# A sorted piece of 131072 edges in two pieces of 65536, the first of them gathered while the second is sorted

## The chip, the cores and the metric

The kernel runs on one core of a Trainium2 chip. The core has a matrix engine (PE, with its weight loads shown as PEld), a vector engine (DVE), a scalar engine (ACT), a general engine (POOL) and a queue engine (SP). Each engine takes its own instructions in a written order and waits for others through semaphores. SP, ACT and POOL also issue DMAs, each in the order of its own queue; a gather or a scatter by a list of row numbers (an indirect DMA) is issued by POOL. The time is device microseconds of one execution. Before the change it is 2055.23 us, the median of 11 runs from 2052.35 to 2058.8.

## The reference, cut to what matters

```python
edge_index = jnp.stack([src, dst])            # 200000 edges, 6250 nodes, D = 256
xn = _layernorm(x)
neigh = xn[dst]                               # one row of 256 for every edge
w = sigmoid(relu(neigh @ W1 + b1) @ W2 + b2)
num = segment_sum(neigh * w, src)             # per node: weighted sum of its edges' rows
den = segment_sum(w, src)
x = x + where(den > 0, num / max(den, 1e-12), 0) + mix(xn)
x = x + ffn(layernorm(x))                     # 6 experts of 3 layers, all run, the best 2 summed
```

The weight of an edge depends on its `dst` node alone, so the kernel makes a row of `xn * w` with `w` and a 1 behind it once for each node, and the edges only have to gather and add these rows. `mix` is an attention without softmax: one 32 by 32 matrix for each of 8 heads, summed over all nodes, and then applied to each node.

## The kernel before, in words

The nodes make 49 tiles of 128, in 13 groups of 4 tiles, and 25 blocks of 2 tiles (the block is what `blk` counts). A row of the table `y_rows` holds three bf16 terms of 258 numbers, whose sum is close to float32.

The edges come sorted by `dst`. They are cut into ranges that are treated differently:

- Edges 0 to 65535 (the piece "b", `hot`) end in the first nodes. They are sorted by source, and for each block a matrix of counts is made of comparisons (L964, L966), with products on PE (L973, L992). Nothing is gathered for them.
- Edges 65536 to 196607 (the piece "a", `cold`, 128 rows of 1024) are sorted by source with a bitonic sort on DVE (L250, L265, L266: one step is a minimum and a maximum over half the elements); between phases the data is turned on PE and copied back by ACT (L301, L302). The sorted list is written to memory, and for each block a window of it is loaded back: 44 columns of 128 edges, of which half 0 of the block uses columns 0 to 22 and half 1 uses columns 19 to 43. One column and half makes one *cold step*: a gather of 128 rows (L728, once for each column), a comparison on DVE that makes a 128 by 128 matrix `hot1` (L736), and three products on PE that add the rows to the node tile's sum `pu` (L750). There are 1175 cold steps and 1079 gathers.
- The last 3392 edges (`few`) are not sorted. For each of 27 lots of 128 edges, rows are gathered (L492), edges with equal source are added up by a product (L508), copied (L512), and added to a table in memory by a scatter (L513). Each scatter waits for the one before it, since both add to the same table.

The instructions are put in order by a planner written in the kernel: a `Line` is a generator that issues some instructions and yields the estimated busy time and a wait; `run` takes the first line in a list that is due. With this the program is laid out in two parts.

*The first part.* SP loads the piece's edges, all of `x` into one tile `xn_all` (L395), the few edges, and zeroes the table with 50 writes (L420), in this order. Then run, one beside the other: the statistics of the 49 node tiles on DVE (`deviations`, L431 and L432), the rows of `y_rows` in two interleaved lines of groups (`node_rows`), the sort of "a", the 27 few lots (`few_edges`) once the node rows are done, and what fits of the sort of "b". After the sort of "a" the first window is decoded, and a second loop places one cold step after another with `heads` (the sums for `mix`: L838, L844, L856), the rest of the sort of "b" and `equal_keys` beside them. Gathers are made 10 steps ahead (`AHEAD`) into 24 buffers (`GBUF`). This loop ends when all of those lines are done.

*The second part.* The class `Work` goes through the groups: `node_terms` (L1017), the count matrices of the blocks, the sums, the normalisation and the router, and the experts (L1145, L1162). One cold step is placed, then as much of this work as a running credit allows, so that 150 us of work (`LAST`) is left when the cold steps end. A cold step is not placed while `HELD - 2` finished sums wait for their block.

Of the kernel before, what the change touches and what calls it, by code (L numbers as in the profile page):

```python
# [20 lines left out]
GT = 4  # L21
# [6 lines left out]
GBUF = 24  # L28
AHEAD = 10
HELD = 16  # L30
# [19 lines left out]
def kernel(  # L50
# [61 lines left out]
    cold = [Piece("a", 65536, 1024, P, 44, 23, 19)]  # L112
# [79 lines left out]
    sq_ps = sps.__enter__()  # L192

    sp_small = ctx.enter_context(tc.tile_pool(name="srt", bufs=1))
    srt = tc.tile_pool(name="srt_a", bufs=1)
    sp_large = srt.__enter__()
# [8 lines left out]
    def pool_of(p):  # L205
        return sp_large if p.row == 1024 else sp_small
# [98 lines left out]
    def merged(p, k, m):  # L305

        t = turned(p, k, "t", False)
        yield 0, TURN[p.name]
# [12 lines left out]
        yield 0, TURN[p.name]  # L321
# [9 lines left out]
    TURN = {"a": 3500.0, "b": 2300.0, "c": 1600.0}  # L331
# [5 lines left out]
    def sort(p, between=()):  # L337
# [3 lines left out]
        for step_between in between:  # L341
            step_between()
# [18 lines left out]
    def starts_of(i0, i1):  # L361
        n = i1 - i0
# [9 lines left out]

    xn_pool = tc.tile_pool(name="xn", bufs=1, side="right")
    xnp = xn_pool.__enter__()
    xn_all = xnp.tile([P, NTILE, D], FP, name="xn_all")
# [18 lines left out]
    for g, t0, nt, rows, r in groups:  # L394
        nc.sync.dma_start(xn_all[:r, t0 : t0 + nt], x[t0 * P : t0 * P + rows].rearrange("(t p) d -> p t d", p=r))  # L395
# [28 lines left out]
    def deviations():  # L424
# [3 lines left out]
        for t in range(NTILE):  # L428
            r = rows_of(t)
            st = nw.tile([P, 6], FP, name="st", bufs=2)  # L430
            nc.vector.bn_stats(st[:r], xn_all[:r, t])  # L431
            nc.vector.bn_aggr(mv[:r, t], st[:r])  # L432
            yield 500, 0
# [50 lines left out]
    def few_edges():  # L484
# [3 lines left out]
        def gather(i):  # L488
            if i < NFEW:
                r = min(P, E - FEW - i * P)  # L490
                gt = nw.tile([P, TERMS, W], BF, name="gt_c", bufs=3)
# [28 lines left out]

    def node_rows(line):

        for g, t0, nt, rows, r in groups[line::2]:
            xg = xn_all[:r, t0 : t0 + nt]
# [37 lines left out]
            sq = nw.tile([P, CB, GT * P], FP, name=f"sq{line}")  # L562
            nc.scalar.activation(sq[:, 0, :rows], dev[:, :rows], AF.Square)
            nc.tensor.matmul(dev[:, :rows], centre, xnT[:, :nt, 1, :r], start=True, stop=True)

# [10 lines left out]
            nc.scalar.activation(sq[:, 1, :rows], dev[:, :rows], AF.Square)  # L576
            for j in range(nt):
                for c in range(CB):
                    nc.tensor.matmul(  # L579
                        ph[:r, P + (j * CB + c) * HB4 : P + (j * CB + c + 1) * HB4],  # L580
                        sq[:, c, j * P : j * P + r], head_of, start=True, stop=True,
                    )
# [48 lines left out]
    ORDERED = {getattr(mybir.EngineType, e) for e in ("PE", "DVE", "Activation", "Pool", "SP")}  # L631
    line_s = Line(counts(0))
    line_t = Line(few_equals(), before=[line_s])
    line_d = Line(deviations())
    lines_y = [Line(node_rows(i), before=[line_d]) for i in range(2)]
    line_c = Line(few_edges(), before=lines_y + [line_t])
    line_a = Line(sort(cold[0], [lambda: starts_of(0, 1)]))
    line_u = Line(counts(1), before=lines_y)
    line_b = Line(sort(hot))
    with tc.manual_schedule(engines=ORDERED):  # L640
        clock[0] = 4000.0
        run([line_s, line_a], 20000.0)
        first_lines = [line_s, line_d] + lines_y + [line_c, line_t, line_a]
        while any(a.open for a in first_lines):
            run(first_lines + [line_u, line_b], clock[0] + 1000.0)
    n_work.__exit__(None, None, None)
    srt.__exit__(None, None, None)
    xn_pool.__exit__(None, None, None)

# [763 lines left out]
```

## Time and profile before

| | |
|---|---|
| median of 11 runs | 2055.23 us (2052.35 to 2058.8) |
| the profiled execution's own time | 2055.01 us |
| its span, first to last instruction | 2053.2 us |
| mean granted PE clock | 0.915 |
| first gather of the cold steps issued at | 401.8 us |
| first `node_terms` result taken by DVE (second part begins) | 511.9 us |
| last gather issued at | 1828.1 us |
| busy: PE, DVE, POOL, ACT | 86%, 63%, 54%, 26% of the span |

The profile is one execution. It lists the busy time of each engine in equal slices and in chosen windows, groups of instructions by line and shape with the mean time of one, the waits in front of them, and the chain of work that ended last. The line numbers are those of the kernel before unless said otherwise. The mean of one instruction runs from its start to its end; where instructions follow each other, the next starts before the last has ended, so the distance from start to start is shorter.

### The profile page before, as it was taken

What the parts mean: (1) busy time and instruction counts of PE and PEld (TensorE: products, weight loads), DVE (VectorE), ACT (ScalarE), POOL (GpSimd) and SP (SyncE); (2) the same over time, 40 slices, a digit from 0 to 9 for tenths busy, and PEclk for the clock granted to TensorE, in tenths of its full rate; (3) what the DMA queues carried; (4) which work ended last, traced back from release to release, by engine and by line L of the source; (5) the groups of instructions that cost most, each with busy time, mean ns of one, the idle gap of its engine ahead of it and who ended that gap; (6) DMA issues with size and microseconds to landing.
All of it is one profiled execution on the core that took longest, in us unless ns stands there. A gap on an engine that the chain in (4) does not pass through costs nothing.

```text
span 2053.2 us, 29846 instructions
## 1 busy us (share of the span) xinstructions
PE 1768.1 (86%) x9751; PEld 1193.0 (58%) x9751; DVE 1300.5 (63%) x5161; ACT 531.4 (26%) x1037; POOL 1111.8 (54%) x1146
## 2 busy tenths in 40 slices
PE   0888332396888999999999999999999999999997
PEld 0555222274554676666766666666666666666555
DVE  8987899677874555566655556655656565565321
ACT  6665431000111212212121221312122122222332
POOL 0000255277777777776776767677676767740000
PEclk9866555598897999999999999999999999999999
DMA  9432233397666666565665656566565565640000
GB/s 245 136 114 93 58 62 65 96 289 228 176 165 179 164 167 193 154 190 145 178 171 150 189 145 186 147 161 190 151 192 140 156 178 157 193 99 18 1 11 14
DMA packets 148725, 294.83 MB, mean 144 GB/s; under 512 B 27914, under 2 KB 94483, under 8 KB 148563
## 3 DMA queue, kind: packets, MB, share of 16 engines
q0 software_dynamic: 74592, 222.62, 40.9%
q1 hardware_dynamic: 63719, 64.97, 10.0%
q10 hardware_dynamic: 10252, 5.27, 1.0%
q8 instruction: 78, 1.28, 0.3%
q14 instruction: 84, 0.69, 0.1%
HBM read 259.37 MB, written 33.40 MB: 143 GB/s over the span
## 4 chain that ended last, share of the span: by engine, by line
PE 76%; DVE 10%; DMA 7%; issue 3%; ACT 3%; POOL 0%; POOLq 0%; SPq 0%; DVEq 0%; ACTq 0%
PE px L1145 24%; PE pu L750 17%; PE px L1162 12%; PE ph L973 6%; PE ph L992 5%; DMA table<-sm,few_row 5%; PE ph L546 2%; PE px L1132 1%; PE ph L579 1%; DMA gt<-y_rows,dsts 1%; PE ph L1017 1%; PE px L1052 1%; DVE k_a L265 1%; DVE fr L966 1%; PE ph L856 1%
## 5 line engine op out<-in xcount | busy, mean ns | idle before, releaser
L728 POOL DMA_INDIRECT gt<-y_rows,dsts x1079 | 1033.8, 958 | 420.6 <-issue 153.7
L750 PE MATMUL pu<-gt,hot 128*128 128x258 bf16 x3525 | 576.5, 278 | 12.6 <-DMA gt<-y_rows,dsts 11.3
L750 PEld LDWEIGHTS <-hot 128*128 128x128 bf16 x3525 | 346.4, 99 | 343.2 <-issue 273.6
L966 DVE TENSOR_SCALAR fr<-count,rdl 128x128 bf16<-128x128 bf16 x1105 | 274.3, 273 | 95.5 <-PE ph L973 94.7
L1154 ACT ACTIVATE h<-px,eb_t 128x512 f32<-128x512 f32 (+1 forms) x312 | 206.6, 662 | 434.6 <-PE px L1145 433.7
L1145 PE MATMUL px<-fT,ew_t 128*128 128x512 f32 (+1 forms) x624 | 298.2, 573 | 0.3 <-ACT fT L1046 0.3
L1145 PE MATMUL px<-h,ew_t 128*128 128x512 f32 (+1 forms) x624 | 296.9, 570 | 0.0
L1162 PE MATMUL px<-ew_t,h 128*128 128x256 f32 (+1 forms) x1176 | 296.7, 380 | 0.0
L736 DVE TENSOR_SCALAR hot<-count,loc 128x128 bf16<-128x128 bf16 x1175 | 272.1, 271 | 24.9 <-PE pu L750 23.5
L1171 DVE SCALAR_TENSOR_TENSOR acc<-px,gate,acc 128x256 f32<-128x256 f32 (+1 forms) x294 | 128.5, 477 | 180.5 <-PE px L1162 180.5
L973 PE MATMUL ph<-to,fr 128*128 128x256 bf16 x1105 | 224.4, 280 | 18.0 <-DVE fr L966 15.8
L1162 PEld LDWEIGHTS px<-ew_t,h 128*128 128x128 f32 (+1 forms) x1176 | 203.4, 190 | 24.9 <-issue 4.3
L964 DVE TENSOR_SCALAR to<-count,hloc 128x256 bf16<-128x256 bf16 x562 | 168.2, 302 | 3.1 <-PE ph L973 3.1
L973 PEld LDWEIGHTS <-fr 128*128 128x128 bf16 x1105 | 108.3, 98 | 65.4 <-DVE fr L966 41.9
L975 ACT CAST cn<-ph 128x256 bf16<-128x256 f32 x150 | 55.8, 372 | 328.2 <-PE ph L973 322.5
L992 PE MATMUL ph<-yh,cn 128*128 128x258 bf16 x882 | 130.8, 273 | 0.0
L783 POOL IOTA last_first<- 128x6 f32 x1 | 0.2, 152 | 219.5 <-DVE rest L588 219.5
L1002 DVE TENSOR_TENSOR cs<-ph,cs 128x258 f32<-128x258 f32 x49 | 20.9, 427 | 153.4 <-PE ph L992 152.7
L1145 PEld LDWEIGHTS px<-fT,ew_t 128*128 128x128 f32 x624 | 96.4, 191 | 22.0 <-issue 14.7
L1145 PEld LDWEIGHTS px<-h,ew_t 128*128 128x128 f32 x624 | 95.7, 190 | 21.6 <-issue 17.1
L992 PEld LDWEIGHTS <-cn 128*128 128x128 bf16 x882 | 85.7, 97 | 15.4 <-issue 2.0
L265 DVE TENSOR_TENSOR k_a<-k_a 128x512 f32<-128x512 f32 x115 | 79.4, 691 | 4.8 <-ACT k_a L302 1.8
(227 smaller groups left out, 1668.3 us busy)
## 6 DMA issues: line engine op xcount, KB each, us to landing
gt<-y_rows,dsts POOLq DMA_INDIRECT x1079
y_rows<-ys SPq DMA_DIRECT2D x10, 774.0 KB
table<-zero SPq DMA_DIRECT2D x50, 129.0 KB
tb<-table SPq DMA_DIRECT2D x49, 129.0 KB
xn_all<-in_x_dram SPq DMA_DIRECT2D x12, 512.0 KB
xnT_d<-xnT SPq DMA_DIRECT2D x12, 512.0 KB
xt<-xnT_d SPq DMA_DIRECT2D x12, 512.0 KB
u<-in_x_dram SPq DMA_DIRECT2D x12, 512.0 KB
```

Source lines behind the costliest of these rows:

```text
L265: nc.vector.tensor_tensor(lo, a, b, op=ALU.min)
L728: nc.gpsimd.indirect_dma_start(out=gt.rearrange("p k w -> p (k w)"), out_offset=None, in_=y_rows, in_offset=bass.IndirectOffsetOnAxis(ap=d ...
L736: nc.vector.tensor_scalar(hot1, count[:, half * P : (half + 1) * P], loc[:, j : j + 1], None, op0=ALU.is_equal)
L750: nc.tensor.matmul(self.pu, hot1, gt[:, k], start=(start and k == 0), stop=(stop and k == TERMS - 1))
L964: nc.vector.tensor_scalar(made[j1], count, loc[:, j1 : j1 + 1], None, op0=ALU.is_equal)
L966: nc.vector.tensor_scalar(fr, count[:, :P], rdl[:, d1, j1 : j1 + 1], None, op0=ALU.is_equal)
L973: nc.tensor.matmul(pa, matrices[i], made[j], start=(j == j0), stop=(j == j1 - 1))
L992: nc.tensor.matmul(pu[:, :W], cn[:, d, s * P : (s + 1) * P], yh[:, d, k], start=(d == 0 and k == 0), stop=(d == HOT - 1 and k == TERMS - 1),)
L1145: nc.tensor.matmul(ph[:, :rows], w[:, e, c, f * P : (f + 1) * P], ins[:, c, :rows], start=(c == 0), stop=(c == CB - 1),)
L1154: nc.scalar.activation(h[:, f, :rows], ph[:, :rows], AF.Relu, bias=bc)
L1162: nc.tensor.matmul(po[:r, j - j0], h2[:, c, j * P : j * P + r], ew_t[2][:, e, c, :], start=(c == 0), stop=(c == CB - 1),)
L1171: nc.vector.scalar_tensor_tensor(acc[:r, j, :], po[:r, j - j0], gate[:r, j, e : e + 1], acc[:r, j, :], op0=ALU.mult, op1=ALU.add)
```

## The change

The piece "a" becomes two pieces "a" and "c" of 128 rows of 512. Each has windows of 23 columns, of which half 0 uses columns 0 to 11 and half 1 uses columns 9 to 22.

The order of cold steps becomes a list of `passes`. The first 4 blocks (`LEAD`) are gone through from "a" alone, then the same 4 blocks from "c" alone, where the partial sums kept in `parts` are added by DVE, and from block 4 on each block is gone through from both windows together. The second piece's sort is finished, in the written order, at the latest when the first window of "c" is loaded (`piece_sorted`).

The few edges leave the first part: they are now a line beside the first cold steps, and use the cold steps' gather buffers. A new loop places one cold step for every 2200 ns of planned time until they are done; then the expert weights are loaded (now on SP's queue, no longer on ACT's), and the old loop goes on with 1300 ns until the sorts of "c" and "b", `heads` and `equal_keys` are done.

`xn_all` goes. `x` is loaded group by group, once for `deviations` and once more for `node_rows` (`x_load`, four buffers of a group). These loads are issued where `deviations` begins, which is after the 50 table writes on SP's queue. The squares for the heads share the buffer `hT`, so the products of the first half of a row (`squares`) come before the second half is squared. `GBUF` goes from 24 to 22, `HELD` from 16 to 18.

```diff
-    cold = [Piece("a", 65536, 1024, P, 44, 23, 19)]
+    cold = [Piece("a", 65536, 512, P, 23, 12, 9), Piece("c", 131072, 512, P, 23, 12, 9)]
...
-    for g, t0, nt, rows, r in groups:
-        nc.sync.dma_start(xn_all[:r, t0 : t0 + nt], x[t0 * P : t0 * P + rows].rearrange("(t p) d -> p t d", p=r))
+    def x_load(g):
+        if g >= len(groups):
+            return None
+        _, t0, nt, rows, r = groups[g]
+        xs = nw.tile([P, GT, D], FP, name=f"xs{g % 2}", bufs=2)
+        nc.sync.dma_start(xs[:r, :nt], x[t0 * P : t0 * P + rows].rearrange("(t p) d -> p t d", p=r))
+        return xs
...
+    passes = [(blk, [p]) for p in cold for blk in range(LEAD)] + [(blk, cold) for blk in range(LEAD, NBLK)]
...
             if stop:
+                blk, ps = passes[i]
+                t = blk * SB + half
+                if ps == cold[1:]:
+                    self.sums[t] = self.parts.pop(t)
+                    nc.vector.tensor_tensor(self.sums[t], self.pu, self.sums[t], op=ALU.add)
+                else:
+                    (self.sums if ps == cold else self.parts)[t] = cs = csp.tile([P, W], FP, name="cs")
+                    nc.scalar.copy(cs, self.pu)
...
     with tc.manual_schedule(engines=ORDERED):
-        clock[0] = 4000.0
-        run([line_s, line_a], 20000.0)
-        first_lines = [line_s, line_d] + lines_y + [line_c, line_t, line_a]
+        clock[0] = 8000.0
+        line_u[1].before = line_u[2].before = lines_y
+        first_lines = [line_d] + lines_y + [line_u[0], line_a, line_t]
         while any(a.open for a in first_lines):
-            run(first_lines + [line_u, line_b], clock[0] + 1000.0)
+            run(first_lines + [line_u[1], line_h, line_a2, line_u[2], line_b], clock[0] + 1000.0)
+        starts_of(0)
...
+        cold_edges = Cold(lambda p: p is cold[0] or piece_sorted(p))
+        beside = [line_c, line_u[1], line_h, line_a2, line_u[2], line_b, line_e]
+        run(beside[1:], clock[0] + 9000.0)
+        cold_edges.decode(0)
+        run(beside[1:], clock[0] + 2000.0)
+        due = clock[0]
+        while line_c.open:
+            cold_edges.step()
+            clock[0] += 200.0
+            due = max(due + 2200.0, clock[0])
+            run(beside, due)
...
-                nc.scalar.dma_start(t[:, e], w[e].rearrange("(c p) h -> p c h", p=P))
+                nc.sync.dma_start(t[:, e], w[e].rearrange("(c p) h -> p c h", p=P))
```

## The prediction

> **What bounds the kernel now.** I read the slices first, then the busy time of the engines in windows cut at the events of the program (end of the statistics, last node row, first gather, start of the second part, first expert, last gather), then the groups, then single stretches.
>
> The second and fifth part of the page, and the busy time in windows (columns: length, PE, PEld, DVE, ACT, POOL, granted clock, DMA share, GB/s):
>
> ```profile
> PE   0888332396888999999999999999999999999997
> DVE  8987899677874555566655556655656565565321
> POOL 0000255277777777776776767677676767740000
> ...
> 25.00:51.00 26.00, 0.02 (x1) 0.05 (x1) 24.33 (x100) 19.32 (x32) 0.00 (x0) 1.00 0.93 246
> 51.00:225.00 174.00, 139.19 (x557) 95.49 (x558) 147.78 (x340) 100.78 (x201) 0.15 (x1) 0.74 0.32 108
> 225.00:402.00 177.00, 50.71 (x210) 36.23 (x209) 150.27 (x303) 43.83 (x102) 76.51 (x55) 0.53 0.35 66
> 402.00:512.00 110.00, 83.43 (x636) 71.18 (x636) 83.01 (x270) 6.21 (x13) 84.48 (x84) 0.89 0.82 253
> 512.00:645.00 133.00, 105.88 (x682) 70.43 (x682) 92.09 (x476) 14.21 (x39) 98.89 (x104) 0.81 0.61 169
> 700.00:1855.00 1155.00, 1150.51 (x6622) 768.98 (x6621) 694.91 (x3272) 260.57 (x500) 808.59 (x848) 1.00 0.60 164
> ```
>
> Two parts with two limits are to be seen. From 645 us PE is full (1150.5 of 1155), so there only PE work counts. Up to 512 us DVE is the fullest, 425 us busy in all; PE's spare time there is worth something only if DVE's work, which must be over before the second part, ends earlier.
>
> The groups, SP's queue, the first gathers on POOL, DVE pairs of a sort step, and a stretch of the chain:
>
> ```profile
> L728 POOL DMA_INDIRECT gt<-y_rows,dsts x1079 | 1033.8, 958 | 420.6 <-issue 153.7 <-PE ph L973 106.5 <-PE pu L750 81.6
> L513 POOL DMA_INDIRECT table<-sm,few_row x27 | 47.0, 1740 | 59.5 <-DMA table<-sm,few_row 27.8 <-ACT sm L512 26.3 <-issue 2.0
> L492 POOL DMA_INDIRECT gt_c<-y_rows,dst_c x27 | 29.3, 1086 | 17.1 <-DMA y_rows<-ys 9.2 <-issue 7.3 <-PE pT L508 0.6
> ...
> 7.10 20.02 SPq L395 DMA_DIRECT2D xn_all<-in_x_dram  x13
> 31.27 28.73 SPq L420 DMA_DIRECT2D table<-zero  x49
> ...
> 404.44 0.95 POOL L728 DMA_INDIRECT gt<-y_rows,dsts  x1 [0.30 <-issue]
> 405.69 0.95 POOL L728 DMA_INDIRECT gt<-y_rows,dsts  x1 [0.30 <-issue]
> ...
> 379.67 0.69 DVE L265 TENSOR_TENSOR k_a<-k_a 128x512 f32<-128x512 f32 x1
> 381.00 0.69 DVE L265 TENSOR_TENSOR k_a<-k_a 128x512 f32<-128x512 f32 x1
> 384.32 0.43 DVE L265 TENSOR_TENSOR k_b<-k_b 128x256 f32<-128x256 f32 x1
> 385.12 0.43 DVE L265 TENSOR_TENSOR k_b<-k_b 128x256 f32<-128x256 f32 x1
> ...
> 563.87 10.38 PE pu L750 x93
> ```
>
> Gathers follow each other every 1.26 us (404.44 to 405.69), nearly all of it POOL's own time; a product of a cold step takes 0.112 us (10.38 / 93); a sort step (a minimum and a maximum) takes 1.33 us at 512 elements and 0.80 at 256.
>
> **The change, step by step.** I follow it to the moment when DVE takes the first `node_terms` (511.9 us before), then add the second part.
>
> *1. Start.* In the changed order the first 98 working instructions of DVE are the statistics, ahead of the first sort step. Their `x` loads are now behind the 50 table writes on SP. Before, SP is done with the piece loads at 7 us; the few loads take 3 us (27.2 to 30.2), the writes 50 x 0.59 = 29 us (28.73 / 49), and a load needs some 3 us to land: first statistics at 43 us. If the writes go at their issue time alone (0.44 us, 22 us) it is 36. DVE, which before did 20 us of sort and set-up by 25 us, stands until then, and the sort of "a" is queued behind it. The statistics take the 26 us of the window 25:51: over at 69 us (before 51).
>
> *2. Node rows.* Before 174 us (51 to 225). Their work on PE and ACT is unchanged but for the second loading of `x` (prefetched a group ahead, behind stores on SP; nothing while a pair of groups takes 174 / 6.5 = 27 us) and the shared `hT`. In this stage DVE had 171 sort instructions of 512 elements and 46 of 256; now it has 248 of 256: 97 us for 132, so 35 less. PE is at 139 of 174 with a clock of 0.74, so I give little of it: 168 (140 if DVE set the pace, 185 if the shared `hT` costs 1.5 us a group). Last row at 237.
>
> *3. To the first gather.* Of the sorts, 146 instructions of 256 elements are left ahead of the first `hot1`, with the first of `heads`: 61 us of DVE time by the groups' means. At the 85% of the window 225:402 it is 72 (65 to 85 at 94% and 72%): first gather at 309, not 402. What goes here is the serial tail of the long sort; what is late next is POOL.
>
> *4. Few edges beside gathers.* Until the last scatter POOL issues 71 cold gathers (1.26 us), 27 few gathers (1.09 + 0.30) and 27 scatters (1.74 + 0.30): 89 + 38 + 55 = 182 us. DVE has 148 us of work in the same stretch, mostly the sort of "c". The wait for the scatter before is now behind 2.6 gathers, 3.3 us, against 5 us from scatter to scatter before, so it mostly goes; but a scatter that waits for its ACT copy now holds the cold gathers behind it on POOL, then the `pu` products on PE, then `hot1` on DVE. I take 190. Bounds: 157 if a scatter costs what a gather costs and DVE fills the time; 224 if the period of 5 us stays and the gathers come on top (135 + 89).
>
> *5. To the second part.* The sort of "b" is left: 76 us of DVE time and 56 gathers (70 us). The window 402:512 had 83 in 110 us, with its 10 us tail of loading the list back. I take 90 (81 to 100).
>
> Sum: 43 + 26 + 168 + 72 + 190 + 90 = 589, against 512: **+77 us**. The lower ends give 36 + 26 + 140 + 65 + 157 + 81 = 505, the upper 43 + 28 + 185 + 85 + 224 + 100 = 665.
>
> DVE's total agrees: 425 us before; two sorts for one (272 steps x 0.80 = 218 for 153 x 1.33 = 203) +15, 60 more `hot1` at 0.17 to 0.27 us +13, decodes and partial sums +5, makes 458, and with 36 us lost at the start 494 without any other wait; before, the other waits were 80.
>
> *6. Second part.* Windows overlap: 26 steps for each window and block instead of 48 for the block, 1272 steps in all for 1175. 133 are done when it begins (before 73), so 1139 are left for 1102: 37 x 3 x 0.112 = +12 us of PE work. Gathers left are even (1128 - 127 = 1001 for 1079 - 75 = 1004), so POOL does not become the bound. The first expert product stands 80 cold steps behind the start, before 123. In that stretch (512:645) steps wait for gathers and PE lost 27 us; a third less of it gives back 10. Together **+2**.
>
> *7. At nothing.* Expert loads on SP: 18 issues while SP waits; ACT's loads for the router wait until the last few lot is through, some 5 us of ACT, which is idle 94% of the window 402:512. POOL's `last_first` (L783, waiting 219.5 us harmlessly before) now stands among the gathers until the last scatter has landed, at most the 5 us of a scatter, inside the bounds of step 5. `GBUF` 22: gathers are only 10 steps ahead.
>
> The Trainium skill, VectorE: DVE Perf Modes, section "The TRN2 errata", speaks against halving a piece: a float32 two-tensor operation takes (N + 151) / 0.96 ns, 424 for 256 elements and 691 for 512. These are the rows' durations to the nanosecond or two, but 544 x 424 - 306 x 691 would make the split +19 us, while the distances from start to start above make it +15: the overlap hides part of the fixed cost. The sum would be 4 us longer by the rule.
>
> The profiled execution has 2055.01 us, 0.2 below the median. 2055 + 77 + 2 = **2134 us**.
>
> **The rivals.**
>
> *A. Faster.* DVE, with three independent sorts to choose from, hardly ever waits, and the early gathers are a gain. For it: between 225 and 402 DVE was held by products of few edges in PE's order, and these stretches are now filled. The second part must begin before 510; by DVE alone it can at 494, and with everything else on time this gives 2055 - 18 + 2 = 2039. Against it: POOL alone needs 182 + 70 us after the first gather, so that must be out by 258, where 309 is my sum. Chance 0.06.
>
> *B. No difference.* Nearly all the lower ends of steps 1 to 5 together: a second part that begins between 506 and 514 us. Chance 0.03.
>
> *C. Half of it.* DVE was the pace of the node rows, and 35 us less sort there shorten them to 140, and the writes go at 0.44 us: 2134 - 28 - 7 = 2099. For it: DVE's 85% in that window. Against: PE's 80% at a low clock, and that PE's instructions in turn wait for ACT. Chance 0.2.
>
> *D. The scatters hold the gathers.* POOL's queue is in order, and with 5 us from scatter to scatter plus gathers step 4 takes 224, and the node rows 185: 2134 + 34 + 17 = 2185. For it: 26 of 59 us of idle time before the scatters was for ACT's copy. Chance 0.2.
>
> *My forecast*, between C and D: 0.51.
>
> **How the numbers follow.** The changed medians of this kernel can be told apart from about 0.2%, 4 us. Slower by more: forecast, C and D, 0.91; same 0.03; faster 0.06. The range goes from somewhat below C to D: 2082 to 2190, leaving out A, B and the ends of C and D.
>
> **What would show it.** Step 1: DVE idle from about 4 to 43 us, waiting for an `x` load, SP's writes ahead of it. Step 2: last `ys` near 237. Step 3: first cold gather near 309. Step 4: last scatter near 499, gathers 1.26 us apart between scatters, POOL above 85%. Step 5: first `node_terms` near 589. Step 6: PE full soon after, 3816 products instead of 3525, last gather about 80 us later. I am wrong if the statistics begin before 30 us, if the node rows take under 140, or if the second part begins before 510 us.

## The result and the profile after

The changed kernel takes 2142.66 us (median of 8 runs, 2140.32 to 2146.04), the kernel before on the same chips 2055.97 (31 runs): a ratio of 1.0421, 95% interval 1.041 to 1.0432. So it is slower by 4.2%. The forecast was 2134 (2082 to 2190) and slower. The profiled execution of the changed kernel took 2146.0 us, its span is 2144.2 (before: 2055.01 and 2053.2), and the mean granted PE clock is 0.907 (before 0.915).

The slices of the page of the changed kernel:

```profile
PE   0488637644568999999999999999999999999998
DVE  1776987995878565565566655565556656555322
POOL 0000006777756677777676777777777777760000
```

The dense part of POOL's row (6s and 7s) begins two slices earlier than before, where the 2 5 5 2 ahead of it were the few edges. DVE begins with nearly nothing (1, then 7 7 6). The lasting 9s of PE begin in the same slice as before, but a slice is 53.6 us long now (51.3 before), and the slices ahead of it are emptier (4 5 6 8, before 6 8 8 8): PE is full later. The last reading is the one that decides the time.

The busy time in windows cut at the same events as in the forecast (columns: window and length, then busy time and instructions of PE, PEld, DVE, ACT and POOL, granted clock, DMA share, GB/s):

```profile
0.00:46.40 46.40, 0.00 (x0) 0.00 (x0) 2.38 (x27) 1.28 (x1) 1.60 (x12) 1.00 0.85 208
46.40:72.40 26.00, 0.00 (x0) 0.00 (x0) 24.26 (x99) 0.00 (x0) 0.00 (x0) 1.00 0.70 224
72.40:254.00 181.60, 148.51 (x556) 103.05 (x556) 132.80 (x396) 118.08 (x248) 0.00 (x0) 0.70 0.37 121
254.00:322.00 68.00, 21.61 (x111) 18.79 (x112) 59.11 (x164) 23.94 (x56) 0.00 (x0) 0.58 0.12 38
322.00:518.00 196.00, 117.41 (x696) 88.32 (x694) 160.67 (x507) 40.83 (x101) 145.74 (x125) 0.69 0.61 140
518.00:610.00 92.00, 43.65 (x229) 31.20 (x229) 65.19 (x221) 7.41 (x16) 66.30 (x69) 0.65 0.76 225
714.00:1942.00 1228.00, 1223.74 (x7096) 820.45 (x7094) 726.45 (x3415) 273.02 (x520) 874.61 (x920) 0.99 0.61 167
```

The windows are the forecast's six stages: 46.4 us in which DVE does 2.4 us of work; the statistics; node rows; DVE's tail of the first sort (59 of 68 us); the first gathers with the few edges (DVE 161 and POOL 146 of 196); the rest of the sort of "b". Behind them PE is full again.

SP's queue and DVE at the start (start, duration, engine, line, operation, tiles; in brackets the idle time before it and what ended it):

```profile
12.69 27.62 SPq L426 DMA_DIRECT2D table<-zero  x50
40.35 33.36 SPq L399 DMA_DIRECT2D xs<-in_x_dram  x17
...
46.47 0.43 DVE L438 BATCH_NORM_STATS2 st<-xs 128x6 f32<-128x256 f32 x1 [42.98 <-DMA xs<-in_x_dram]
```

The loads of `x` are behind the 50 writes, and DVE stands 43 us for the first of them.

The groups of gathers and scatters (busy time, mean ns of one, then idle time before them and what ended it):

```profile
L836 POOL DMA_INDIRECT gt<-y_rows,dsts x1128 | 1079.3, 957 | 747.0 <-DVE srcs L781 320.0 <-issue 165.9 <-PE pu L861 108.9
L521 POOL DMA_INDIRECT table<-sm,few_row x27 | 46.4, 1719 | 20.5 <-ACT sm L520 9.3 <-issue 8.7 <-ACT t_b L306 1.9
L500 POOL DMA_INDIRECT gt<-y_rows,dst_c x27 | 27.7, 1026 | 8.2 <-issue 6.1 <-PE pu L861 1.2 <-PE pT L516 0.3
```

A stretch of POOL's timeline in the stage with the few edges:

```profile
391.84 1.70 POOL L521 DMA_INDIRECT table<-sm,few_row  x1 [0.30 <-issue]
393.85 0.98 POOL L500 DMA_INDIRECT gt<-y_rows,dst_c  x1 [0.30 <-PE pu L861]
395.13 1.07 POOL L836 DMA_INDIRECT gt<-y_rows,dsts  x1 [0.30 <-issue]
396.51 0.95 POOL L836 DMA_INDIRECT gt<-y_rows,dsts  x1 [0.30 <-PE pu L861]
397.76 0.99 POOL L836 DMA_INDIRECT gt<-y_rows,dsts  x1 [0.30 <-issue]
399.06 1.64 POOL L521 DMA_INDIRECT table<-sm,few_row  x1 [0.30 <-issue]
```

And of the waits in the same stage, those of a scatter for its copy (us in total, times, longest):

```profile
POOL table L521 <- ACT sm L520: 9.3, 1, 9.3
```

The 59.5 us that scatters waited before are 20.5. The wait for the scatter before is gone from the group, and only one scatter held POOL for long for its ACT copy, for 9.3 us.

When the last scatter is through (it ends at 518.3 us), ACT issues the loads for the router; ACT's and DVE's rows there:

```profile
497.74 0.58 ACT L306 COPY k_b<-turn 128x512 f32<-128x512 f32 x1 [0.41 <-PE turn L305]
520.25 0.43 ACTq L902 DMA_DIRECT2D rw_t<-in_L_ffn_router_w_dram  x1
521.94 0.58 ACT L306 COPY t_b<-turn 128x512 f32<-128x512 f32 x1 [23.61 <-DMA eb_t<-in_L_ffn_expert_b_dram]
...
522.55 0.90 DVE L254 SCALAR_TENSOR_TENSOR t_b<-t_b 128x128 f32<-128x128 f32 x4 [12.88 <-ACT t_b L306]
```

A copy of the sort of "b" (`t_b`) stands behind these loads in ACT's order. So ACT does nothing for 23.6 us, and DVE stands for 12.9 us in the middle of that sort.

The marks of all kernels that follow, from their traces (us; the last column is what is left of the span from the first expert product on):

| kernel | first statistics | last node row | first gather | first `node_terms` | first expert product | from there to the end |
|---|---|---|---|---|---|---|
| before | 24.8 | 224.5 | 401.8 | 511.9 | 645.5 | 1408 |
| after | 46.5 | 253.8 | 322.2 | 610.0 | 714.6 | 1430 |
| table writes later | 16.4 | 223.7 | 292.1 | 579.4 | 683.9 | 1430 |
| counts on ACT earlier | 45.9 | 244.8 | 313.1 | 600.1 | 703.8 | 1428 |
| few edges first | 46.4 | 255.0 | 452.7 | 576.6 | 711.4 | 1431 |
| `LEAD` 0 | 46.7 | 255.7 | 442.9 | 663.7 | 795.3 | 1430 |
| split only | 25.5 | 210.0 | 420.1 | 513.0 | 675.4 | 1433 |
| before, experts earlier | 24.5 | 223.7 | 400.9 | 511.0 | 597.5 | 1440 |

With the split pieces the time in this table is the first expert product plus 1428 to 1433 us, whatever came before: the stage behind that mark gives nothing back.

### The profile page after: what moved, and what is told of

It reads as the page before. It is cut to its first block, busy times and chain, and to the rows that moved or that the text cites. A ratio compares the mean times of both kernels' runs of the same rounds, so it can differ in the third digit from the quotient of the medians.

```text
span 2144.2 us, 31189 instructions
## 1 busy us (share of the span) xinstructions
PE 1833.8 (86%) x10048; PEld 1242.9 (58%) x10048; DVE 1328.8 (62%) x5546; ACT 537.7 (25%) x1088; POOL 1155.2 (54%) x1195
## 4 chain that ended last, share of the span: by engine, by line
PE 67%; DVE 4%; issue 0%; DMA 0%; ACT 0%; POOL 0%; DVEq 0%
PE px L1186 23%; PE pu L861 17%; PE px L1203 12%; PE ph L1014 5%; PE ph L1033 5%; PE px L1173 1%; DVE fr L1007 1%; PE ph L1058 1%; PE px L1093 1%; DVE to L1005 1%; PE px L1086 0%; PE px L1099 0%; PE pT L770 0%; DVE hot L844 0%; DMA gt<-y_rows,dsts 0%
## 5 line engine op out<-in xcount | busy, mean ns | idle before, releaser
L836 POOL DMA_INDIRECT gt<-y_rows,dsts x1128 | 1079.3, 957 | 747.0 <-DVE srcs L781 320.0
L861 PE MATMUL pu<-gt,hot 128*128 128x258 bf16 x3816 | 633.2, 285 | 9.8 <-DMA gt<-y_rows,dsts 9.1
L861 PEld LDWEIGHTS <-hot 128*128 128x128 bf16 x3816 | 385.1, 102 | 352.8 <-issue 269.1
L844 DVE TENSOR_SCALAR hot<-count,loc 128x128 bf16<-128x128 bf16 x1272 | 293.6, 272 | 18.2 <-PE pu L861 17.3
L1014 PE MATMUL ph<-to,fr 128*128 128x256 bf16 x1105 | 224.5, 280 | 18.2 <-DVE fr L1007 13.4
L552 PE MATMUL turn<-ident,xs 128*128 128x128 f32 (+1 forms) x98 | 28.2, 425 | 85.9 <-ACT xs L543 82.1
L552 PEld LDWEIGHTS turn<-ident,xs 128*128 128x128 f32 (+1 forms) x98 | 18.5, 215 | 94.6 <-issue 77.8
```

The lines of the kernel that those rows point to most:

```text
L836: nc.gpsimd.indirect_dma_start(out=gt.rearrange("p k w -> p (k w)"), out_offset=None, in_=y_rows, in_offset=bass.IndirectOffsetOnAxis(ap=d ...
L844: nc.vector.tensor_scalar(hot1, count[:, half * P : (half + 1) * P], loc[:, j : j + 1], None, op0=ALU.is_equal)
L861: nc.tensor.matmul(self.pu, hot1, gt[:, k], start=(start and k == 0), stop=(stop and k == TERMS - 1))
L1014: nc.tensor.matmul(pa, matrices[i], made[j], start=(j == j0), stop=(j == j1 - 1))
```

## The experiments

My theory after the result: the loss is made of a late start (the table writes ahead of `x`), of more cold steps by the overlapping windows, and of a stage of few edges and first gathers that POOL's queue sets. The rivals were that the delays at the start are hidden later, that the extra steps are paced by gathers and not by PE, and that DVE sets that stage. Where nothing else is said, the kernel before takes 2057 to 2060 us (medians) on the chip of the run, and the ratio is to it.

**1. Table writes later.** In the changed kernel the writes stand behind the stores of the node rows, four for a group.

```diff
-    for t in range(TROWS // P):
-        nc.sync.dma_start(table[t * P : (t + 1) * P], zero)
+    to_zero = list(range(TROWS // P))
...
+            for t in to_zero[g * 4 : g * 4 + 4]:
+                nc.sync.dma_start(table[t * P : (t + 1) * P], zero)
```

> The changed kernel, with the 50 table writes moved from ahead of the first x loads to behind the stores of the node rows, four to a group. Theory (the first part is one chain that starts with the statistics): the first statistics start at about 17 us instead of 46.5, everything up to the experts follows, 2143 - 29 = 2114 us. Rival 1 (the first part ends when DVE has done its total work, and the start is only one place for its idle time): some of the gain is lost again to waits in the node rows, 2125 to 2135. Rival 2 (the first part is paced by POOL and the scatters alone): the first gather moves but the time does not, 2138 to 2143.

Measured: 2113.4 us, ratio 1.0259 (1.0222 to 1.0295).

```profile
16.38 0.43 DVE L437 BATCH_NORM_STATS2 st<-xs 128x6 f32<-128x256 f32 x1 [12.89 <-DMA xs<-in_x_dram]
```

The statistics begin 30.1 us earlier, and every later mark moves by 30 to 31 us: last node row, first gather, `node_terms`, expert, span (2113.5 for 2144.2). No stage behind the start had any slack to hide it.

**2. Counts on ACT earlier.** ACT counts how many edges of piece "a" lie below the start of each block (`counts`, tile `junk_a`). In the changed kernel the planner placed these counts among the node rows; here their line stands first in the list.

```diff
-        first_lines = [line_d] + lines_y + [line_u[0], line_a, line_t]
+        first_lines = [line_u[0], line_d] + lines_y + [line_a, line_t]
```

> The changed kernel, with the counting of the first piece's sources (24 ACT operations of 0.72 + 0.19 us) placed beside the statistics, where ACT stands idle, instead of among the node rows. Theory (the node rows took 182 us instead of the forecast 168 because ACT got these 22 us): stage of the node rows 168 to 172 us, 2143 - 12 = 2131 us. Rival (the shared buffer of the squares, or the second load of x, is what lengthened the stage): 2139 to 2143.

Measured: 2132.6 us, ratio 1.0357 (1.0322 to 1.0392). The groups on ACT during the node rows of the changed kernel, and the window of the node rows in this run:

```profile
L355 ACT ACTIVATE junk_a<-src_a,thr 128x512 bf16<-128x512 int32 x24 | 17.3, 719 | 0.5
L355 ACT ACTIVATION_READ_ACCUMULATOR junk_a<-src_a,thr 128x1 f32 x24 | 4.5, 188 | 0.0
```

```profile
71.70:245.00 173.30, 146.13 (x556) 101.28 (x556) 132.73 (x396) 100.00 (x200) 0.00 (x0) 0.70 0.39 128
```

ACT has 18 us less work in the stage, and the node rows take 173 us instead of 182. The span falls by 12.4 us, the median by 10. DVE's work there is the same (132.7), so DVE is not the pace of the node rows: this speaks against rival C's reason.

**3. Few edges first.** The few edges are gathered and scattered as soon as the node rows are there, ahead of the cold gathers, as before the change; early blocks and pieces stay as changed.

```diff
-    line_c = Line(few_edges())
+    line_c = Line(few_edges(), before=lines_y + [line_t])
...
-        first_lines = [line_d] + lines_y + [line_u[0], line_a, line_t]
+        first_lines = [line_d] + lines_y + [line_c, line_u[0], line_a, line_t]
```

> The changed kernel with one part undone: the few edges again run after the node rows beside the sort, not beside the first cold gathers. Theory (POOL's queue sets when the experts begin: 188 gathers for 213 cold steps, and with the change 27 gathers and 27 scatters among them): few edges from 254 to about 390 us, first cold gather at about 395, first expert product at 395 + 188 x 1.26 + some 20 = 650 instead of 714 us, 2143 - 60 = 2083 us, and the sort of the second piece goes on beside them. Rival (the part is the gain that its words suggest, since scatters and gathers fill POOL's gaps): the first gather comes over 70 us later and the time grows to 2170 or more.

Measured: 2138.6 us, ratio 1.0374 (1.0327 to 1.042), not to be told from the changed kernel. Both expectations were wrong. POOL's timeline of this run at the first two scatters, and PE's around their products:

```profile
291.66 1.90 POOL L521 DMA_INDIRECT table<-sm,few_row  x1 [25.40 <-ACT sm L520]
301.41 1.59 POOL L521 DMA_INDIRECT table<-sm,few_row  x1 [6.56 <-ACT sm L520]
```

```profile
275.45 1.08 PE L305 MATMUL turn<-ident,t_a 128*128 128x128 f32 x4 [5.48 <-DVE few_eq L477]
284.47 1.08 PE L305 MATMUL turn<-ident,k_a 128*128 128x128 f32 x4 [7.93 <-DVE k_a L270]
285.35 0.85 PE L516 MATMUL pT<-gt,few_eq 128*128 128x258 bf16 x3
297.29 1.08 PE L305 MATMUL turn<-ident,t_a 128*128 128x128 f32 x4 [11.09 <-DVE t_a L270]
298.16 1.91 PE L679 MATMUL dv<-centre,xt 128*128 128x128 f32 x8
299.87 0.85 PE L516 MATMUL pT<-gt,few_eq 128*128 128x258 bf16 x3
```

What held the scatters, in total (us, times, longest):

```profile
POOL table L521 <- ACT sm L520: 57.5, 9, 25.4
POOL table L521 <- DMA table<-sm,few_row: 21.7, 10, 3.0
POOL table L521 <- ACT junk_b L355: 10.7, 5, 3.2
```

PE takes the few products in its written order, behind turns of the sort (`turn`) that wait for DVE; the copy and the scatter wait for the product. ACT's counts (`junk_b`, `junk_c`) and the scatter before hold a scatter too, but less. So a scatter costs 5.5 us (27 in the 148 us from 291.7 to 440.0), and the first cold gather, for which I had expected 395, comes at 452.7. From it to the first expert product there are then 259 us, as expected. The few lots ahead of the gathers cost as much as they save behind them.

**4. No early blocks.** `LEAD` is 0: no block is gathered from "a" alone, so that the sort of "c" is over before the first gather. The few edges stay beside the gathers.

```diff
-LEAD = 4
+LEAD = 0
```

> The changed kernel with LEAD = 0: no block is gathered from the first piece alone, so the first cold gather waits for the sort of the second piece. Theory (POOL is late in the first part, so an earlier first gather is worth its time): first gather some 80 us later, about 400 us, experts about 50 us later, 2143 + 50 = 2193 us. Rival (DVE's total work decides, and the order of the gathers within it does not matter): 2135 to 2155 us.

Measured: 2219.95 us, ratio 1.078 (1.0743 to 1.0817): 74 to 77 us slower than the changed kernel, more than I had expected. The window from the end of the first sort to the first gather:

```profile
322.00:443.00 121.00, 25.90 (x123) 19.84 (x123) 88.52 (x248) 16.20 (x35) 0.05 (x1) 0.54 0.04 12
```

POOL does nothing for 121 us, and the DMA engines are at 0.04. So the early blocks do fill that time, where the few edges have left it.

**5. Windows without overlap.** Half 0 of a block uses columns 0 to 11 and half 1 columns 12 to 22, so 1128 cold steps for 1272, with the same 1128 gathers. Edges that lie on the other side of column 12 are left out; the kernel counts its edges, finds some missing and goes through all of them again in a slow way, which is why the whole takes 25404 us. So only the trace up to the end of the second part is read.

```diff
-    cold = [Piece("a", 65536, 512, P, 23, 12, 9), Piece("c", 131072, 512, P, 23, 12, 9)]
+    cold = [Piece("a", 65536, 512, P, 23, 12, 12), Piece("c", 131072, 512, P, 23, 12, 12)]
```

> The changed kernel with the two halves of a window split at column 12 without overlap: 46 cold steps for a block instead of 52, 1128 in all instead of 1272, with the same 1128 gathers. Edges that lie on the other side of column 12 than their node tile are left out of the sums. Theory (from the first expert product on PE is full, and a cold step costs its three products of 0.112 us there): first expert product at cold step 187 instead of 213 but after as many gathers (187 for 188), so at the same 714 us; then 941 steps for 1059, 118 x 0.336 = 40 us less, 2143 - 40 = 2103 us. Rival (the gathers pace the second part): 2140 to 2143, as the gathers stay.

Measured: the flag that ends the second part (`bad`) is written at 2098.8 us, in the changed kernel at 2137.0, so 38 us less. Behind the first expert product it is 32.7 us for 118 steps, 0.277 us each, though the gathers are as many. On PE the products of cold steps take 38.8 us less there (0.33 us a step, near the forecast price of 0.336), and other products 6 us more; why they do was not traced. PE sets the price of a step there, and not the gathers.

**6. Split only.** The kernel before with the one piece of 1024 columns as two of 512, and nothing else of the change.

```diff
-    cold = [Piece("a", 65536, 1024, P, 44, 23, 19)]
+    cold = [Piece("a", 65536, 512, P, 23, 12, 9), Piece("c", 131072, 512, P, 23, 12, 9)]
...
-    line_a = Line(sort(cold[0], [lambda: starts_of(0, 1)]))
+    line_a, line_a2 = Line(sort(cold[0])), Line(sort(cold[1]))
+    line_a2.before = [line_a]
```

The planned wait for a turn of the sort, and the lists that place the second sort, follow the split.

> The kernel before with only the split of the large piece into two (windows of 23 columns each, 52 cold steps for a block); both are sorted ahead of the first gather, the few edges, the x loads and the table writes stand as before. Theory: DVE has 15 us more of sort steps, first gather at about 417 us; first expert product at cold step 213, after 188 gathers instead of 180, at 670 us for 645; from there 1430 us for 1408; 2055 + 25 + 22 = 2102 us. Rival (the split itself is nearly free and the loss is in the start and the order): below 2075 us.

Measured: 2102.7 us, ratio 1.0217 (1.02 to 1.0234), so 46 us. The second part begins when it did before (513.0 for 511.9), though DVE has 8.6 us more work up to there (433.9 for 425.3) and the first gather comes 18 us later (420.1 for 401.8, forecast 417). What gives way is the steps: 10 fewer are done when the second part begins (63 for 73). Between there and the first expert product are 150 for 123, and 29 us more; behind it 1059 for 979, and 25 us more. These 55 us are of the profiled execution, which took 7 us more than the median.

**7. Before, experts earlier.** In the kernel before, the second part places cold steps and other work by a running credit; where a step of that other work finds nothing that is due (`took is None`), the chain of operations that leads to the experts (normalisation and router) is not looked at either, and is placed too late. Here `spend(0.0)` looks at it, and places its next operation if that is due.

```diff
                 if took is None:
+                    work.spend(0.0)
                     credit = 0.0
```

> The kernel before, where the planner of the second part also lets the router chain of a group go on when the sums wait for a block's cold steps (one call more; no work is added or left out). First expert product at cold step 150 instead of 196. Theory (the stretch before the first expert is paced by gathers while PE idles 27 us of 133): first expert at 645 - 42 x 1.26 = 592 us, and half or more of the 27 us comes back: 2035 to 2045 us. Rival (PE's idle time there comes from the chain's own waits, not from gathers): 2052 to 2057 us.

Measured: 2041.37 us, ratio 0.993 (0.9914 to 0.9947): faster than both kernels. The first expert product stands at cold step 150 in the order, 196 before, and comes at 597.5 us for 645.5. PE's rows from there on:

```profile
512.00:597.00 85.00, 72.58 (x480) 49.57 (x478) 68.81 (x364) 11.56 (x32) 62.28 (x67) 0.83 0.61 171
597.00:1816.00 1219.00, 1207.98 (x6981) 806.65 (x6980) 727.67 (x3424) 273.73 (x524) 883.83 (x929) 0.99 0.61 169
```

PE's waits for gathers in the kernel before, from 512 to 645 us (us, times, longest):

```profile
PE pu L750 <- DMA gt<-y_rows,dsts: 11.0, 19, 1.3
PE pu L750 <- DVE hot L736: 1.3, 2, 1.0
```

PE idles 12 us ahead of the experts where it idled 27, and in that stretch its products of cold steps (`pu`) no longer wait for a gather. The gain is the steps moved from where they wait to where PE is full. Some products of the count matrices moved with them.

**8. The changed kernel with 1, 2 and 7.** All three edits in one kernel.

> The changed kernel with the table writes behind the node rows' stores, the first piece's counts beside the statistics, and the router chain let go on as in the run above. First expert product at cold step 197 instead of 213. Theory: gains of the first two add up (30 + 11), the third gives some 10: 2143 - 51 = 2092 us, still above the kernel before. Rival (with the start mended the change is worth its gain): 2055 us or less.

Measured: 2093.64 us, ratio 1.0173 (1.0156 to 1.019). The second part begins at 570.1 us for 610.0, about the sum of experiments 1 (30.6) and 2 (9.9), and the first expert product comes 84 us behind that instead of 105. With start and planner mended the change still loses 1.7% to the kernel before, which has neither edit.

**9. Without the few edges, twice.** The changed kernel without the gathers, products, copies and scatters of the 27 few lots; the rest and the planned pace stay (the kernel's own count of the edges is set to match).

```diff
-        gather(0)
-        gather(1)
         for i in range(NFEW):
-            gather(i + 2)
             yield 0, 4500
-            r, gt = got.pop(i)
-            ps = p_t.tile([P, GT * P], FP, name="pT")
-            for k in range(TERMS):
-                nc.tensor.matmul(
-                    ps[:r, :W], few_eq[:r, i, :r], gt[:r, k], start=(k == 0), stop=(k == TERMS - 1)
-                )
...
-            nc.scalar.copy(sm[:r], ps[:r, :W])
-            nc.gpsimd.indirect_dma_start(
-                out=table,
...
```

> The changed kernel without the work of the few lots: their 27 gathers, products, copies and scatters are left out (so 3392 edges are missing from the sums); all else, the planned pace of the cold steps too, stays. The kernel with the change has its first gather at 322.2 us, the first expert product at 714.6, and 1430 us from there to the end. Theory (POOL's queue sets the pace between the first gather and the end of the few edges): POOL loses 27 x (0.99 + 0.30) + 27 x (1.63 + 0.30) = 87 us, and the experts begin about that much earlier, at 625 to 640, so about 2055 to 2070 us. Rival (DVE sets the pace, POOL's work lies beside it): DVE has some 175 us of sort and comparisons left between the first gather and the end of the sort of c where the stage takes 196, so at most 25 us are to be had: experts at 690 or later, 2118 us or more.

Measured: 2399.9 us on a chip where the kernel before takes 2317.3; ratio 1.0339 (1.0298 to 1.038). The second run:

> The same kernel once more (the work of the few lots left out), since the chip of the run before took 2317 us for the kernel before the change, all of the surplus after 400 us, where its engines wait for 'issue'. In the changed kernel DVE is busy for 141.8 of the 159 us from the first gather to the end of the sort of c (322 to 481), and for 76.9 of the last 81. Theory now (DVE sets that stretch; POOL alone only the 37 us behind it, up to the last scatter): first gather at 322 to 325, the sort of c over by 470 to 480, experts 10 to 25 us earlier than 714.6, total 2118 to 2132 us where the kernel before takes 2055, a ratio of 1.031 to 1.037. Rival (POOL sets it, and the late chip hid the gain): experts at 640 or earlier, 2070 us or less, ratio under 1.008.

Measured: 2372.25 us, on another such chip (before: 2305.2); ratio 1.0302 (1.0233 to 1.0371). Two windows of the changed kernel, and one of the second run without the few edges:

```profile
322.00:400.00 78.00, 60.08 (x439) 52.94 (x437) 64.82 (x200) 20.78 (x53) 54.54 (x48) 0.89 0.67 168
400.00:481.00 81.00, 41.90 (x182) 25.32 (x182) 76.93 (x248) 16.80 (x41) 63.41 (x54) 0.54 0.57 119
```

```profile
324.00:490.00 166.00, 88.10 (x551) 70.38 (x549) 141.96 (x449) 29.41 (x70) 73.59 (x73) 0.72 0.39 112
```

POOL has 74 us of work in place of 118, DVE the same 142, and the sort of "c" ends no earlier (489.6 us; 480.8 with the few edges; I had expected 470 to 480). DVE's wait for the keys of a window, which it takes in its written order, is 18.1 us there for 10.7. By the ratios 17 to 25 us of 2055 are gained (8 to 39 by their intervals), where POOL as the bound would have given some 87. My first theory falls: up to the end of the sort of "c" it is DVE that sets the pace (142 of 159 us, and 77 of the last 81), and POOL sets at most the 37 us behind it, up to the last scatter. Part of the gain is not POOL's time at all: without the few lots ACT issues the router's loads at 277 us, and the 12.9 us in which DVE stood behind them do not occur. As both chips are late behind 400 us (see the last section), the middle of the trace is not exact to 10 us, and that the ratios carry over to the other chips is assumed: the changed kernel itself was not run on a late one.

**10. The kernel before with its table writes first.** Only the order of SP's queue is changed; DVE's order stays, with the sort first.

```diff
+    zero = nw.tile([P, W], FP, name="zero")
+    nc.vector.memset(zero, 0.0)
+    for t in range(TROWS // P):
+        nc.sync.dma_start(table[t * P : (t + 1) * P], zero)
     for g, t0, nt, rows, r in groups:
         nc.sync.dma_start(xn_all[:r, t0 : t0 + nt], x[t0 * P : t0 * P + rows].rearrange("(t p) d -> p t d", p=r))
...
-    zero = nw.tile([P, W], FP, name="zero")
-    nc.vector.memset(zero, 0.0)
-    for t in range(TROWS // P):
-        nc.sync.dma_start(table[t * P : (t + 1) * P], zero)
```

> The kernel before with one edit: the 50 table writes stand ahead of the loads of x on SP's queue, as they do in the changed kernel; the order of DVE stays, so the sort is beside the loads. The writes take 22 to 28 us, so the first statistics come at about 47 us instead of 24.8. Theory (the late start is paid whole, sort beside it or not, because the sort work that DVE has up to 25 us is all that its order puts ahead of the statistics): second part 18 to 22 us later, about 2073 to 2078 us. Rival (the sort of the large piece fills the gap, since what is delayed is not what ends last before the second part): within 5 us of 2055.

Measured: 2337.89 us where before takes 2317.3; ratio 1.008 (1.0054 to 1.0106). The two windows of the start:

```profile
0.00:25.00 25.00, 0.00 (x0) 0.00 (x0) 19.91 (x62) 15.18 (x24) 1.61 (x12) 1.00 0.88 212
25.00:44.00 19.00, 0.00 (x0) 0.00 (x0) 0.01 (x1) 17.18 (x27) 0.00 (x0) 1.00 0.94 238
```

DVE's first statistics in the timeline:

```profile
43.99 0.43 DVE L431 BATCH_NORM_STATS2 st<-xn_all 128x6 f32<-128x256 f32 x1 [19.40 <-DMA xn_all<-in_x_dram]
```

DVE does its 20 us of sort and then stands for 19 us, since the statistics are next in its order. The first gather comes 18.5 us later (420.3 for 401.8), and the whole 20. So this order on the queue costs 16 to 21 us (by the ratio, or as measured on this late chip) also where DVE has sort work to begin with. Experiment 1 gave 30 because the changed kernel has none ahead of its statistics.

**11. Before, experts earlier still.** Experiment 7, with each cold step before the first expert counted as 1260 ns of planned time, so that the experts stand at cold step 132.

```diff
-                work.now += TERMS * BFNS
+                work.now += 1260.0 if work.begun < 0 else TERMS * BFNS
```

> The kernel before with work offered to the credit after every cold step that finishes no block (as in the run that took 2041 us), and with each cold step before the first expert counted as 1260 ns, the distance of gathers, instead of the time of its three products. The experts then stand at cold step 132 in the order instead of 150 (196 in the kernel before). Theory (every cold step ahead of the experts that is moved behind them saves the wait for its gather, 13.9 us for 46 steps in the last run, so 0.30 us each): 18 steps give 5 us, 2036 us. Rival (the rest ahead of the experts is set by DVE and the count products, not by gathers): same as the last run, 2039 to 2043.

Measured: 2303.62 us where before takes 2317.3; ratio 0.9942 (0.9915 to 0.9968). That is the ratio of experiment 7, not the 0.9907 of the theory (2036 / 2055), so no further gain is shown; the interval excludes the theory's 5 us, but not one of 3.

## Why the prediction was right, and where its steps were not

The direction, and 91% for slower, rested on a second part that begins later: 610.0 us measured, 589 forecast, 511.9 before. The total was 8.7 us too low. That it came so near is in part luck: the second part began 21 us later than forecast and then took 9 us less, and the two misses have opposite signs.

- *Step 1 (start at 43, statistics over at 69)*: 46.5 and 72.2. The writes took 27.6 us, as taken from the rows of before; the first statistics began 6 us behind the issue of their load, where the forecast had 3, a term that none of its rows shows. Experiment 1 shows that this order is worth 30 us.
- *Step 2 (node rows 168)*: 181.6, the largest miss, 14 us. "Their work on PE and ACT is unchanged" was the step that failed: the 24 counts of piece "a", 22 us of ACT, had been done at the start before, while ACT had nothing else, and now stood among the rows. Experiment 2 gives 8 of the 14 us back. The remaining 5 were not traced. DVE's work in the stage fell by 15 us (147.8 to 132.8), not by 35; that this would not shorten the stage was right.
- *Step 3 (72)*: 68.4, with DVE at 87% of it.
- *Step 4 (190)*: 196, inside its bounds, but for another reason than mine. I summed POOL's 182 us and let DVE lie beside it. With 0.30 us ahead of each, POOL's 125 gathers and scatters did fill 183 us. But DVE had 161 us in the stage, not 148, and experiment 9 shows that it sets most of it. The scatter's wait for the scatter before went, as said, and rival D's wait for ACT's copy was there once, 9.3 us.
- *Step 5 (90)*: 92, with 65 us of work on DVE, not 76, and part of the wait of step 7 in it.
- *Step 6 (+2)*: -7 (1541.3 us from `node_terms` to the end before, 1534.2 now). The price of a step beside the experts was right: from the first expert product to the last cold step there are 80 more steps and 27.3 us more, 0.34 us each, for 3 x 0.112 = 0.336. The waits were right too: PE waited 12.3 us for gathers and `hot1` between the second part's begin and the experts, now 0.6, where 10 less was forecast. Two terms were missing. The 43 steps fewer in that stretch also save their products, 20.8 us, which take longer there (0.42 us a step before, at a granted clock of 0.81; beside the experts it is 1.00). With the waits that is 32 us; other products lose 3 again, and the stretch is 29 us shorter. And the time behind the last cold step is 5.4 us shorter (193.7 us for 199.1), with 4.8 us less idle time on PE. Together 27.3 - 29 - 5.4 = -7.
- *Step 7 (nothing)*: here the forecast failed. ACT's loads for the router do wait for the last scatter, as said, but it is not some 5 us of an idle ACT: ACT does nothing for 23.6 us, and DVE, which needs the copy behind them, stands for 12.9. In experiments 1, 2 and 8 the loads are also issued 2 us behind the end of the last scatter, and the same gap on DVE is there (12.7 to 12.9 us); it is not there in the kernel before or in experiment 9. What these loads in another place would be worth was not tested. No wait for the expert weights or `last_first` appears among the larger ones.
- *The cost of the split on DVE (+15 by distances; +19 by the Trainium skill, VectorE: DVE Perf Modes, section "The TRN2 errata")*: sort operations of 256 elements last 418 to 423 ns in the changed kernel (group means), and start 0.34 us (median) or 0.38 (mean) after one another. The page's formula, which it checks at 512 and 2048 elements, makes 424 at 256, by estimate. The traces are nearer to the distances: DVE is busy with operations on the tiles of the sorts of "a" and "c" for 215.8 us, on those of the one sort before for 204.3, so 11.5 us more.
- *Rivals*: A needed a second part before 510 us and got 610. C's node rows (140) and D's (185) lie on both sides of 182, but D's stage 4 (224) did not come.

Where the 87 us come from, by the runs: split alone +46 (more steps), the order of the table writes +30, the counts on ACT +10 to 12. These make 86 to 88 by the medians, and 98 for 91 by the profiled executions. So for all the rest of the change together, the early gathers with the few edges beside them above all, nothing is left over: it gains as much as it costs, to within some 7 us. This is a remainder, not a measurement of one part. The 12.9 us of step 7 are in it as a cost. Experiments 3 and 4 fit it. With neither the few lots nor the first gathers beside the second piece's sort, 74 us are lost (experiment 4); with the few lots alone, as it turned out in experiment 3, the time is that of the changed kernel, which has both there. A reading that the runs allow, but do not show alone: DVE is nearly full there, so the gathers stretch the stage, and the second part begins 33 us later than in experiment 3 (610.0 for 576.6), with 47 more steps done (133 for 86). That is 0.71 us a step, where a step fewer between there and the experts saves 0.67 (29 us for 43 steps, against the kernel before).

## What to carry to other kernels

Before work is moved into a stage because one engine idles there, sum the other engines' work in that stage: here POOL's idle time was real, but DVE was already near full, and the early gathers gained nothing in the end. A change of structure also moves work whose order nobody looked at (writes on a queue, counts on an idle engine), and here that made nearly half of the loss; loads that wait for a late scatter, with a copy behind them, held the fullest engine besides. List each queue's order before and after. When the last stage has a full engine, price every added step by that engine's time per step, and look whether steps can be moved from where they wait into that stage: that gave the only gain here, 0.7%, with one line.

## What the runs showed of the hardware that was not expected

- On two of the chips the kernel before took 2317 and 2305 us instead of 2056. Up to 400 us the marks are the same (first gather at 400.9 us in experiments 7 and 11, on either kind of chip), and so are the durations of single operations (a sort operation of 256 elements 423 ns in both, a gather 956 and 958). Behind that, from `node_terms` to the end, the kernel of experiment 11 took 1753 us and that of experiment 7 took 1527. A stretch of experiment 11 shows how:

```profile
1038.06 0.38 PE L750 MATMUL pu<-gt,hot 128*128 128x258 bf16 x2
1039.32 0.27 PE L750 MATMUL pu<-gt,hot 128*128 128x258 bf16 x1 [0.88 <-issue]
1039.33 0.30 PEld L1145 LDWEIGHTS px<-h,ew_t 128*128 128x128 f32 x2 [1.05 <-issue]
1039.34 0.43 DVE L1002 TENSOR_TENSOR cs<-ph,cs 128x258 f32<-128x258 f32 x1 [9.86 <-remote]
```

  PE stops for 0.88 us between the second and the third product of one cold step, with nothing to wait for that the profile shows, and the other engines start again in the same tenth of a microsecond. The trace has 37 moments of over 0.4 us after 400 us in which no engine is busy, that of experiment 7 none. They make 35 us, a small part of the difference of 226, so most of it lies elsewhere. What stops the engines stays open. Experiments 7 and 11 have nearly the same ratio on the two kinds of chip, but no changed kernel was run on both.
- Sort operations of 256 elements last 0.42 us and start 0.34 us after one another (median); at 512 elements 0.69 and 0.61. The operations that write the tiles of the sorts of "a" and "c" in the changed kernel last 241.8 us in sum, and DVE is busy with them for 214.1: a sum of durations overstates such a chain by an eighth.
